# Layer 2 attention: the transposed sums go ahead of the weighted sums in the first step of a query block

## The chip, the cores and the metric

The kernel runs on one core of a Trainium2 chip. The metric is the device time of one execution in microseconds; the time of a kernel is the median over several executions. A core has five engines with instruction queues of their own: TensorE (PE in the profile, with its weight loads listed apart as PEld), VectorE (DVE), ScalarE (ACT), GpSimdE (POOL) and SyncE (SP, which here only issues DMAs). Each engine runs its queue in order; semaphores make one engine wait for another.

## The reference, cut to what matters

The program is a stack of four layers over x of 8 images of 56 x 56 positions with 128 channels. The change lies in the attention of layer 2, where each image is 3136 tokens. Keys, queries and values are the same projection, so that the matrix of scores is symmetric.

```
kqv = x @ W_k.T
h = kqv.reshape(B, S, HEADS, D_K).transpose(0, 2, 1, 3)      # 8 heads of 16
scores = jnp.einsum('bhqd,bhkd->bhqk', h, h) / jnp.sqrt(jnp.float32(D_K))
attn = jax.nn.softmax(scores, axis=-1)
ctx = jnp.einsum('bhqk,bhkd->bhqd', attn, h)
ctx = ctx.transpose(0, 2, 1, 3).reshape(B, S, D)
t = t + ctx @ W_o.T
```

After it come a normalization, the gate and the choice of tokens for the experts, which the kernel does in the same stage.

## The kernel before, in words

The function `attend` holds the stage. Its order is written out by hand (a manual schedule): each engine gets its instructions in the order in which the code below issues them.

The work is cut into 16 parts `u`: 8 images times 2 groups of four heads. Within a part there are 8 query blocks `b`, taken from 7 down to 0; each is 384 queries wide (`QB`), and block 7 is 448. The keys are cut into tiles of 128; three tiles (`KB`) make a key block `a`. A step is one query block against one key tile, and there are 1856 steps: in each part 25 for block 7 and 13 for each of the blocks 6 to 0.

Because the scores are symmetric, a square of exponentials that was computed for queries `b` and keys `a` serves the pair the other way round too, once it is transposed. So each square is computed once and used twice:

- `scores` (line L1252 of the profile) makes the scores of a step: four matmuls, one for each head, into two of three PSUM buffers `p_s`; ScalarE takes the exponential of each half into `e` (L1260).
- `weigh` (L1305) multiplies the exponentials with the values: four matmuls into the PSUM tile `av`, summed over all the steps of the block. These are the weighted sums. The pool of `av` has one buffer.
- `transpose_squares` (L1271) has VectorE transpose the 32 x 32 squares of `e` into `sq`; `move_squares` (L1287) then issues twelve DMAs on SyncE that move them to other partitions in `x`, and `keep_squares` (L1298) has GpSimdE copy the four that stay on theirs. Each key block so moved is a job.
- `from_squares` multiplies one third of a job with the values: four matmuls, again by `weigh` and so again on L1305, into the PSUM tile `avx`. These are the transposed sums. A job is begun `AGE` = 6 steps after it was made and takes three steps. The tile `avx` shares its one PSUM buffer with the small products of the finishing work (`p_o`, `p_tr`, `p_g`, `p_pool`).
- `take` has VectorE add `av` or `avx` to the block's accumulator (L1324; L1326 and L1328 where it is the first).
- `finish` is the work on a finished block: normalization, the product with W_o (`p_o`, L1366), the transposes (`p_tr`, L1404, evicted on L1405), the gate (`p_g`, L1408, evicted on L1409). It is a generator, advanced one piece in a step by `go_on`.

One matmul of float32 is two instructions in the profile, so that each group of four shows as x8 there.

Within a step `i` the code issues, in this order: the scores of step `i + 1`; the transposes of step `i`; two copies on GpSimdE; perhaps one piece of finishing work; perhaps the next block's queries; the weighted sums of step `i`; if the block ends here, the take of `av`; one third of a job, if one is due; and the DMAs of a job that is complete. So on TensorE a step is: scores, perhaps a small product, weighted sums, transposed sums.

A block's first step (`opens`) begins a new sum in `av`. There the weighted sums must wait until VectorE has taken the last block's sum out of the same PSUM buffer. There are 128 such steps. In 127 of them a job's third is due, by the order of the code: in 111 the first third of a job (the one that waits for the job's DMAs, for GpSimdE's copies and for the buffer of `avx`), in 16 the second third (all in the first step of block 6).

Of the kernel before, what the change touches and what calls it, by code (L numbers as in the profile page):

```python
# [53 lines left out]
AGE = 6  # L54
# [1100 lines left out]
def attend(tc, k, w, low, tok, kT_in, va_in, t_out, gate_w, gate_b, taken, pooled):  # L1155
# [11 lines left out]
    with ExitStack() as ctx:  # L1167
# [23 lines left out]
        def stage(b):  # L1191
            own = [(b, i, m) for i, (_, m) in enumerate(blocks[b][2])]
            if b == last:
                others = [3, 2, 1, 6, 5, 4, 0]
            else:
                others = [(b - r) % last for r in (3, 2, 1)]
                own.append((NQ, 0, S - 128 * (KT - 1)))
            for r, a in enumerate(others):
                yield from [(a, i, 128) for i in range(KB)]
                n_own = -(-len(own) // (len(others) - r))  # L1200
                yield from own[:n_own]
                del own[:n_own]

        steps = [
            (u, b, *step)
            for u in range(len(parts))
            for b in reversed(range(NQ))
            for step in stage(b)
        ]
        keys, queries, exps, squares, sums = {}, {}, {}, {}, {}  # L1210
        jobs, moves, urgent, later = [], [], [], []
# [25 lines left out]
        def make_queries(u, b):  # L1237
            kT, width = keys[u, b][0], blocks[b][1]
            q = wp.tile([128, QB + 64], F32, name="q", bufs=2)
            nc.vector.tensor_scalar(in_order(q), by_square(kT), low, None, ALU.add)  # L1240
            if width > QB:
                nc.vector.tensor_scalar(q[:, QB:width], kT[:, QB:], low, None, ALU.add)
            queries[u, b] = q

        def scores(u, b, a, i, m):

            kT, q, width = keys[u, a][0], queries[u, b], blocks[b][1]
            e = ep.tile([128, 4, QB + 64], F32, name="e")
            ss = [pss.tile([128, 2, 512], F32, name="p_s") for _ in range(2)]
            for j in range(4):  # L1250
                rows = slice(32 * j, 32 * j + 32)
                nc.tensor.matmul(  # L1252
                    ss[j // 2][:m, j % 2, :width],
                    kT[rows, 128 * i : 128 * i + m],
                    q[rows, :width],
                    start=True,
                    stop=True,
                )
            for j in range(2):
                nc.scalar.activation(  # L1260
                    e[:m, 2 * j : 2 * j + 2, :width], ss[j][:m, :, :width], AF.Exp
                )
            exps[u, b, a, i] = e

        def transpose_squares(u, b, a, i):

            if i == 0:
                squares[u, b, a] = tp.tile([128, 4, KB, 4, KB * 32], F32, name="sq")
            sq = squares[u, b, a]
            for j in (0, 2):  # L1270
                nc.vector.transpose(  # L1271
                    sq[:, :, i, j : j + 2].rearrange("p s j c -> p j s c"),
                    exps[u, b, a, i][:, j : j + 2, :QB].rearrange(
                        "p j (s c) -> p j s c", s=4
                    ),
                )

        def move_squares(u, b, a, now):

            sq = squares.pop((u, b, a)).rearrange("p s a j c -> p s (a j c)")  # L1280
            x = xp.tile([128, 4, KB * 4 * KB * 32], F32, name="x")

            for src, dst in (
                *((0, 1), (2, 3), (1, 0), (3, 2), (0, 2), (2, 0)),
                *((0, 3), (2, 1), (1, 2), (3, 0), (1, 3), (3, 1)),
            ):
                nc.sync.dma_start(  # L1287
                    x[32 * dst : 32 * dst + 32, src], sq[32 * src : 32 * src + 32, dst]
                )
            for at in range(4):  # L1290
                rows = slice(32 * at, 32 * at + 32)
                moves.append((x[rows, at], sq[rows, at]))
            jobs.append([u, b, a, x.rearrange("p s (a f) -> p (s a) f", a=KB), 0, now])

        def keep_squares():

            for _ in range(min(2, len(moves))):
                nc.gpsimd.tensor_copy(*moves.pop(0))  # L1298

        def weigh(av, u, b, i, m, e, start, stop):  # L1300
            for j in range(4):
                out = av[32 * j : 32 * j + 32]
                if len(e[j].shape) == 3:
                    out = out.rearrange("p (a i) -> p a i", i=32)
                nc.tensor.matmul(out, keys[u, b][1][:m, i, j, :], e[j], start=start, stop=stop)  # L1305

        def from_squares():
            u, b, a, x, i, _ = jobs[0]
            assert not (i == 0 and len(jobs) == 1 and moves)
            if i == 0:  # L1310
                sums[0] = psm.tile([128, QB], F32, tag="m", name="avx")
            e = [x[:, :, (KB * j + i) * 32 : (KB * j + i) * 32 + 32] for j in range(4)]
            weigh(sums[0], u, b, i, 128, e, i == 0, i == KB - 1)
            jobs[0][4] += 1
            if i == KB - 1:
                jobs.pop(0)
                take(u, a, sums[0])

        def take(u, b, av):

            width = blocks[b][1]
            to = by_square(acc[b])
            if done[b]:
                nc.vector.tensor_tensor(to, to, in_order(av), ALU.add)  # L1324
            else:
                nc.vector.tensor_copy(to, in_order(av))  # L1326
                if width > QB:
                    nc.vector.tensor_copy(acc[b][:, QB:], av[:, QB:width])  # L1328
            done[b] += 1
            if done[b] == (1 if b == last else 5):  # L1330
                work = [finish(*parts[u], b), False]
                urgent.append(work)
                later.append(work)
# [83 lines left out]
        def go_on(work):  # L1417
            try:
                work[1] = next(work[0])
            except StopIteration:  # L1420
                later.remove(work)
# [4 lines left out]
        def reload():  # L1426

            while loads:
                u, b = loads[0]
                n = u - 1  # L1430
                if b < NQ and (
                    not {(n, b), *((n, (b + r) % last) for r in (1, 2, 3) if b < last)} <= used
                    or any(j[:2] == [n, b] for j in jobs)
                ):
                    return
                load_keys(*loads.pop(0))
# [7 lines left out]
        for i, (u, b, a, c, m) in enumerate(steps):  # L1444
            if i + 1 < len(steps):
                scores(*steps[i + 1])
            if a < NQ and a != b:
                transpose_squares(u, b, a, c)
            keep_squares()
            free = not jobs or jobs[0][4] == 0  # L1450
            if urgent:
                go_on(urgent.pop(0))
            elif later and i > turn + 1 and (free or not later[0][1]):
                go_on(later[0])
                turn = i
            if i + 3 < len(steps) and steps[i + 3][:2] != steps[i + 2][:2]:
                make_queries(*steps[i + 3][:2])
            opens = i == 0 or steps[i - 1][:2] != (u, b)
            closes = i + 1 == len(steps) or steps[i + 1][:2] != (u, b)
            if opens:  # L1460
                av = psa.tile([128, 512], F32, tag="av", name="av")
            e = exps.pop((u, b, a, c))
            width = blocks[b][1]
            weigh(
                av[:, :width],
                u,
                a,
                c,
                m,
                [e[:m, j, :width] for j in range(4)],  # L1470
                opens,
                closes,
            )
            if closes:
                take(u, b, av)
                used.add((u, b))
            if jobs and (i - jobs[0][5] >= AGE or i + 1 == len(steps)):
                from_squares()
            if a < NQ and a != b and c == KB - 1:
                move_squares(u, b, a, i)  # L1480
            reload()
# [698 lines left out]
def token_layers(tc, k, a, y, out):  # L2180
# [3 lines left out]
    with ExitStack() as ctx:  # L2184
# [57 lines left out]
        with tc.If(taken > 0) as both:  # L2242
            attend(tc, k, w, low, tok, kT_d, va_d, *dest)
# [100 lines left out]
```

## Time and profile before

| what | value |
|---|---|
| time, median of 3 runs | 7714.85 us (7708.21 to 7727.53) |
| the profiled execution's own time | 7718.14 us |
| its span, first to last instruction | 7716.3 us |
| busy share of the span: PE, DVE, ACT, POOL | 84%, 68%, 54%, 38% |
| the stage of `attend` | from about 1965 us to about 6500 us |
| L1252 scores, PE | 14848 instructions, 548 ns mean |
| L1305 weighted sums into `av`, PE | 14848 instructions, 515 ns mean |
| L1305 transposed sums into `avx`, PE | 10752 instructions, 496 ns mean |
| L1260 exponentials, ACT | 3712 instructions, 830 ns mean |
| L1271 transposes, DVE | 2688 instructions, 950 ns mean |

How to read it: the four matmuls of a group run side by side in the array, and the next group starts before the last has drained, so that the sum of the instructions' times says little; what counts on TensorE is the distance from the start of one group to the start of the next. "Idle" of PE is time in which no matmul was in flight; "idle" of PEld is time between two weight loads, in which matmuls may well be running. PEclk is the share of its clock that TensorE was granted, 1.00 or 0.50 in this stage.

### The profile page before, as it was taken

The page shows a single profiled execution, that of the slowest core. Times are in us where ns is not written, and L with a number is a line of the kernel's source. Part 1 is how long each engine was busy: PE and PEld are TensorE (multiplying, and loading weights), DVE is VectorE, ACT ScalarE, POOL GpSimd, SP SyncE. Part 2 cuts the span into 40 slices and gives each one's busy share as a digit, 9 for nine tenths or more (in the row PEclk, how much of TensorE's full clock was granted, in tenths as well). Part 3 has the DMA queues.
Part 4 walks back from the last instruction along what each step waited for, and adds up shares of the span by engine and source line. Part 5 has one row for each costly group of instructions (what it writes and reads, how often), then busy time and mean ns, then how long its engine had stood idle before and what let it go on. Part 6 is the DMA issues. An engine that isn't in the chain of part 4 may idle for free. (4 is left out here: it accounts for less than half of the span.)

```text
span 7716.3 us, 157926 instructions
## 1 busy us (share of the span) xinstructions
PE 6482.3 (84%) x59883; PEld 2880.7 (37%) x59883; DVE 5284.8 (68%) x9856; ACT 4142.6 (54%) x6467; POOL 2935.1 (38%) x2555
## 2 busy tenths in 40 slices
PE   6659999556899999999999999999999997556654
PEld 4446666334233323323323323333333333245532
DVE  7975564366677777777777777777777776366752
ACT  4424444122666666666666666666666664056740
POOL 0011111022444444444444444444444443434653
PEclk8768898777999999999999999999999998788766
DMA  5453443376788778778778778778778775543543
GB/s 155 137 119 76 86 95 65 82 240 207 199 203 197 193 192 199 189 192 201 191 184 204 188 183 207 183 191 205 185 190 206 182 190 137 196 117 107 134 135 130
DMA packets 736303, 1287.38 MB, mean 167 GB/s; under 512 B 117698, under 2 KB 503108, under 8 KB 728516
## 3 DMA queue, kind: packets, MB, share of 16 engines
q1 hardware_dynamic: 725556, 1260.76, 65.1%
q0 software_dynamic: 6144, 12.60, 0.6%
q8 instruction: 484, 7.93, 0.5%
q10 hardware_dynamic: 3824, 3.68, 0.2%
q14 instruction: 295, 2.42, 0.1%
HBM read 286.04 MB, written 197.81 MB: 63 GB/s over the span
## 5 line engine op out<-in xcount | busy, mean ns | idle before, releaser
L1260 ACT ACTIVATE e<-p_s 128x768 f32<-128x768 f32 (+2 forms) x3712 | 2887.8, 830 | 1584.9 <-PE p_s L1252 1329.8
L1298 POOL COPY x<-sq 32x1152 f32<-32x1152 f32 x1792 | 2059.2, 1149 | 2067.6 <-PE p_s L1252 1330.0
L1271 DVE STREAM_TRANSPOSE sq<-e 128x768 f32<-128x768 f32 x2688 | 2434.5, 950 | 567.3 <-ACT e L1260 312.9
L1252 PE MATMUL p_s<-q,kT 32*128 32x384 f32 (+2 forms) x14848 | 1888.6, 548 | 33.6 <-ACT e L1260 18.6
L1305 PE MATMUL av<-e,va 128*32 128x384 f32 (+2 forms) x14848 | 1645.3, 515 | 30.4 <-DVE acc L1324 20.7
L1305 PE MATMUL avx<-x,va 128*32 128x384 f32 x10752 | 1138.3, 496 | 69.5 <-issue 40.2
L1252 PEld LDWEIGHTS p_s<-q,kT 32*128 32x128 f32 (+1 forms) x14848 | 654.8, 181 | 1252.6 <-issue 825.4
L1305 PEld LDWEIGHTS av<-e,va 128*32 128x32 f32 (+1 forms) x14848 | 294.5, 108 | 1049.4 <-issue 941.7
L1305 PEld LDWEIGHTS avx<-x,va 128*32 128x32 f32 x10752 | 353.2, 111 | 650.9 <-issue 595.2
L609 POOL TENSOR_TENSOR rs<-rs,mhalf 112x4 f32<-112x4 f32 x112 | 116.1, 1036 | 788.3 <-DVE rs L608 788.3
L1324 DVE TENSOR_TENSOR acc<-acc,avx 128x384 f32<-128x384 f32 x336 | 183.9, 547 | 229.9 <-PE avx L1305 228.6
L121 PE MATMUL p_tr<-ident,xn 112*128 112x112 f32 x672 | 134.6, 341 | 187.4 <-DVE xn L112 141.8
L1141 POOL TENSOR_TENSOR rs<-rs,mhalf 112x4 f32<-112x4 f32 (+2 forms) x136 | 168.1, 1236 | 269.3 <-DVE ntop L1942 123.8
L525 ACT COPY wT<-p_w 88x448 f32<-88x448 f32 x152 | 138.0, 922 | 194.1 <-PE p_w L523 161.4
L1990 ACT ACTIVATE xn<-t,ms,rs 112x128 f32<-112x128 f32 x448 | 185.3, 488 | 76.4 <-DVE ms L1983 76.4
L327 DVE SCALAR_TENSOR_TENSOR acc<-xp,dw,acc 128x3136 f32<-128x3136 f32 x56 | 194.3, 3478 | 31.3 <-ACT acc L322 31.2
L637 PE MATMUL p_f<-x1T,w 128*128 128x448 f32 x448 | 205.6, 583 | 4.4 <-DVE x1T L632 2.7
L121 PEld LDWEIGHTS p_tr<-ident,xn 112*128 112x128 f32 x672 | 98.7, 169 | 285.0 <-issue 185.1
L1385 POOL TENSOR_TENSOR rs<-rs,mhalf 128x3 f32<-128x3 f32 (+1 forms) x72 | 58.5, 815 | 365.0 <-DVE rs L1384 343.0
L523 PE MATMUL p_w<-ident,wide 112*88 112x112 f32 x896 | 146.5, 303 | 58.6 <-DMA px<-strips 34.1
L621 DVE TENSOR_TENSOR y<-y,p_rs 128x448 f32<-128x448 f32 x112 | 69.3, 619 | 176.6 <-PE p_rs L614 176.6
L122 ACT COPY xT<-p_tr 128x448 f32<-128x448 f32 x112 | 59.6, 532 | 229.8 <-PE p_tr L121 203.7
(354 smaller groups left out, 7830.9 us busy)
## 6 DMA issues: line engine op xcount, KB each, us to landing
x<-sq SPq DMA_DIRECT2D x5376, 144.0 KB
w<-in_L_ffn_weight_dram SPq DMA_DIRECT2D x64, 1024.0 KB
px<-strips SPq DMA_DIRECT2D x64, 616.0 KB
va_d<-va SPq DMA_DIRECT2D x16, 1600.0 KB
xT_d<-xT SPq DMA_DIRECT2D x112, 224.0 KB
xT<-xT_d SPq DMA_DIRECT2D x112, 224.0 KB
kT_d<-kT SPq DMA_DIRECT2D x16, 1568.0 KB
t<-t_a SPq DMA_DIRECT2D x16, 1568.0 KB
```

Of the source, the lines that this page charges most:

```text
L121: nc.tensor.transpose(p[:, i, :], src[:, i, :], k.ident[:T, :T])
L327: nc.vector.scalar_tensor_tensor(acc, xp[:, j // 3 : j // 3 + IH, j % 3 : j % 3 + IW], dw[:, j : j + 1], acc, ALU.mult, ALU.add,)
L523: nc.tensor.transpose(p[:, g], around[:, :, g], k.ident[:T, :T])
L637: nc.tensor.matmul(p, q.w1[:, f * 128 : (f + 1) * 128], x1T, start=True, stop=True)
L1141: nc.gpsimd.tensor_tensor(rs, rs, k.mhalf[:m, :n], ALU.pow)
L1252: nc.tensor.matmul(ss[j // 2][:m, j % 2, :width], kT[rows, 128 * i : 128 * i + m], q[rows, :width], start=True, stop=True,)
L1260: nc.scalar.activation(e[:m, 2 * j : 2 * j + 2, :width], ss[j][:m, :, :width], AF.Exp)
L1271: nc.vector.transpose(sq[:, :, i, j : j + 2].rearrange("p s j c -> p j s c"), exps[u, b, a, i][:, j : j + 2, :QB].rearrange("p j (s c) -> ...
L1298: nc.gpsimd.tensor_copy(*moves.pop(0))
L1305: nc.tensor.matmul(out, keys[u, b][1][:m, i, j, :], e[j], start=start, stop=stop)
L1324: nc.vector.tensor_tensor(to, to, in_order(av), ALU.add)
L1990: nc.scalar.activation(out[:, i], x[:, i], AF.Identity, bias=ms[:, i : i + 1], scale=rs[:, i : i + 1])
```

## The change

In the first step of a block (but the very first of all), if a job's third is due, `from_squares` is called before the weighted sums and no longer after them. In all other steps nothing is changed. On TensorE the four transposed matmuls and the four weighted ones change places in 127 steps; on the other engines the order of the instructions stays as it was. The number of instructions of computation stays the same.

```diff
             if opens:
+
+                if i and jobs and i - jobs[0][5] >= AGE:
+                    from_squares()
                 av = psa.tile([128, 512], F32, tag="av", name="av")
...
-            if jobs and (i - jobs[0][5] >= AGE or i + 1 == len(steps)):
+            if jobs and not opens and (i - jobs[0][5] >= AGE or i + 1 == len(steps)):
                 from_squares()
```

## The prediction

> **What bounds the kernel now.** The change touches only the stage of `attend`, so I read the table of busy time for that stretch first, then the waits of TensorE, then its timeline around the first steps of blocks.
>
> ```profile
> 1965.00:6500.00 4535.00, 4370.16 (x41569) 1436.31 (x41568) 3411.62 (x4905) 2918.07 (x3814) 2146.77 (x1894) 0.98 0.80 193
> ```
>
> The columns are the stretch, its length, the busy time of PE, PEld, DVE, ACT and POOL, the granted clock, the DMA share and GB/s. TensorE is busy for 4370 of 4535 us and sets the pace: all its idle time is 165 us, and what the change can win is a part of that.
>
> Which part, the waits of that stretch tell (engine, line, releaser: us in total, times, longest). First those of PE, then the one row of PEld that names the same releaser.
>
> ```profile
> PE avx L1305 <- issue: 40.2, 38, 2.2
> PE av L1305 <- DVE acc L1324: 20.7, 15, 2.4
> PE av L1305 <- DVE acc L1328: 8.8, 16, 0.6
> ```
>
> ```profile
> PEld av L1305 <- DVE acc L1324: 74.1, 96, 3.1
> ```
>
> The row of 74.1 us looks like the larger prize and is none: weight loads sit idle while the matmuls before them run. In matmuls the weighted sums lose 20.7 + 8.8, about 30 us in 31 openings. What the other 96 openings look like, a plain one shows (timeline of PE: start, length, line, names, count, idle before and its releaser):
>
> ```profile
> 2947.24 0.94 PE L1252 MATMUL p_s<-q,kT 32*128 32x384 f32 x8
> 2948.11 0.85 PE L1305 MATMUL av<-e,va 128*32 128x384 f32 x8
> 2948.78 0.85 PE L1305 MATMUL avx<-x,va 128*32 128x384 f32 x8
> 2949.57 0.91 PE L1252 MATMUL p_s<-q,kT 32*128 32x384 f32 x6
> ```
>
> From group to group: scores to weighted 0.87 us, weighted to transposed 0.67 us, transposed to scores 0.79 us, with no wait. VectorE has freed `av` before the scores are through. These starts are the prices of the groups: a moved group fills at most some 0.7 us (0.78 in block 7, whose rows are wider).
>
> **The change, part by part.** Only TensorE's order differs, in 127 openings; no DMA is moved, and the queues of SP, POOL, ACT and DVE keep theirs. I went through all 127 in the timeline and sorted them.
>
> *Block 6, 16 openings.* The weighted sums wait for the second copy of block 7's take, L1328:
>
> ```profile
> 2559.69 1.13 PE L1252 MATMUL p_s<-q,kT 32*128 32x384 f32 x8
> 2561.39 0.85 PE L1305 MATMUL av<-e,va 128*32 128x384 f32 x8 [0.57 <-DVE acc L1328]
> 2562.03 0.85 PE L1305 MATMUL avx<-x,va 128*32 128x384 f32 x8
> ```
>
> The moved group is here a job's second third, which waits for nothing. It takes the 0.57 us and the weighted group follows when the buffer is free. Gain 16 x 0.55 = 8.8 us.
>
> *Block 7, 8 openings with a short wait.* Seven wait 0.50 us for L1324, one 0.66: gain 4.2 us.
>
> *Block 7, 7 openings with a long wait.* In them VectorE works on the choice of tokens:
>
> ```profile
> 2783.94 1.15 PE L1252 MATMUL p_s<-q,kT 32*128 32x448 f32 x8
> 2787.46 1.72 PE L1305 MATMUL av<-e,va 128*32 128x448 f32 x8 [2.37 <-DVE acc L1324]
> ...
> 2800.67 0.64 PE L1706 MATMUL p_pool<-expert,chosen 128*128 128x64 f32 x2 [2.19 <-DVE chosen L112]
> ```
>
> The moved group fills 0.78 of the 2.37 us, 5.5 us in all, if TensorE kept it. But 13 us on it waits another 2.2 us for VectorE, and VectorE is idle for only 0.56 us in between. What is won first is mostly waited for later. Between 0 and 5.5 us I take 3 us, near the 7 x 0.56 that VectorE can pass on.
>
> *The plain 74 openings.* Here nothing is hidden that was not hidden before, but the transposed sums now need their input 0.67 us earlier. GpSimdE's copies are done 5.5 us or more ahead in all of them. The DMAs are not: the records of TensorE's semaphore instructions and the ends of the packets put the last piece of a job within some 0.7 us of the weighted group's start in 13 openings. There the transposed group would start 0.1 to 0.95 us late, and the weighted one behind it. Summed one by one: 6 us lost. The bounds are 0, if these pieces come just in time, and 74 x 0.67 = 50 us, if the DMAs keep the pace at every opening; I stay with the sum, because it is read from these very openings. The change of neighbours costs little: weighted to scores takes 0.78 us in steps without transposed sums, against 0.76 for transposed to scores, so 127 x 0.02 = 2.5 us.
>
> *Openings with a gate product, 15, in blocks 5 and 4.* Here the change does harm:
>
> ```profile
> 2625.94 1.10 PE L1252 MATMUL p_s<-q,kT 32*128 32x384 f32 x8
> 2626.97 0.86 PE L1408 MATMUL p_g<-xT,gate 128*64 128x384 f32 x2
> 2627.76 0.85 PE L1305 MATMUL av<-e,va 128*32 128x384 f32 x8
> 2629.26 0.85 PE L1305 MATMUL avx<-x,va 128*32 128x384 f32 x8 [0.64 <-issue]
> 2630.04 0.93 PE L1252 MATMUL p_s<-q,kT 32*128 32x384 f32 x8
> ```
>
> `p_g` and `avx` share one PSUM buffer. `avx` starts 0.10 us after VectorE's eviction on L1409 ends at 2629.16, and that eviction stands behind two transposes (L1271) in VectorE's queue. Today the weighted sums run inside that wait. After the change they are queued behind it on TensorE, with the next scores behind them, and ScalarE's next exponentials wait for those. The transposed group cannot start earlier; the weighted one comes after it: 15 x 0.67 = 10.1 us lost.
>
> *Openings with a transpose, 7, in block 3.* The same with `p_tr` and its eviction on L1405: the transposed group already waits 1.38 us behind the weighted one. The loss is 0.67 less the 0.13 us that the weighted group waits today: 3.8 us.
>
> *The clock.* Idle time has a second price. The long wait above lies in the first of these two stretches (columns as in the table above):
>
> ```profile
> 2783.69:2787.10 3.41, 1.40 (x12) 0.43 (x8) 3.20 (x12) 2.86 (x4) 1.83 (x2) 1.00 0.90 210
> 2787.10:2790.51 3.41, 3.05 (x20) 0.71 (x20) 3.34 (x6) 0.00 (x0) 3.30 (x3) 0.50 0.95 224
> ```
>
> After a stretch in which TensorE was idle for 2.0 of 3.41 us the clock is 0.50 for the next 3.41 us. The stage has 39 such dips, and their starts lie on one grid of 3.41 us. Laying that grid over the stage: all 28 stretches with 1.9 us idle or more are followed by a dip, of those between 1.45 and 1.9 about half, below 1.45 none. A dip takes half of 3.41 us, 1.7 us. In the gate openings the idle stretch grows from about 0.4 to 1.1 us, harmless, but in three it comes to about 1.4 and in one to 2.3: two new dips, to be generous. In block 3 five of seven dip already; with 0.67 us more, all do: two more. Four dips are 6.8 us. That block 7's long waits fall from 2.37 to about 1.6 us may save dips, but what they save is waited for at `p_pool`; I count nothing (the far end is 7 x 1.7 = 12 us gained).
>
> The Trainium skill has a rule on this ("TensorE: Matmul & The Clock Gate", section "Why this matters for your kernels"): no idle gaps over about 3 us between bursts of matmuls. By it no opening here could dip, before or after, and the sum would be 6.8 us smaller. The row above speaks against that threshold: the gap of 2.37 us was enough.
>
> **The sum.** Gains 8.8 + 4.2 + 3 = 16.0. Losses 10.1 + 3.8 + 6 + 2.5 + 6.8 = 29.2. Net 13 us slower: 7718.1 of the profiled execution becomes 7731, and on the median of the runs, 3.3 us lower, 7714.9 + 13 = 7728. A difference of 0.3%, 23 us, is about what a measurement of this kernel can tell from no change; so my forecast is no change, with a lean to slower. With the unknowns at their near ends (no late pieces, no new dips: 0; twice of both: +26) its own range is 7706 to 7738.
>
> **The rivals.**
>
> *The new wait is dearer* (slower, over 0.3%). One mechanism: the wait for the shared PSUM buffer in the 22 openings with a gate product or a transpose, now with nothing in front of it, lengthens TensorE's idle past the point where the clock halves. It decides from 1.9 us idle in one stretch of the grid. If all 15 gate openings dip, not two, that is 13 x 1.7 = 22 us more: 7750. For it: five of seven transposes dip today, at 1.5 to 1.9 us. Against it: 1.1 us in eleven of the fifteen. Chance 0.30.
>
> *The DMAs keep the pace.* All 74 plain openings wait out the 0.67 us: 50 in place of 6, 7772. For it: the DMA share of 0.80 and the 13 late openings. Against it: half of the pieces have landed 1.8 us before. Chance 0.06.
>
> *The gains stand alone* (faster). If evictions came earlier, and block 7 kept its fill and its dips: 8.8 + 4.2 + 5.5 + 12 = 30 us, 7685. Against it: the order on VectorE doesn't change, so the eviction can't come earlier. Chance 0.07.
>
> *The waits row is right.* Whoever adds PEld's 74.1 to the 30 expects 104 us: 7611. The plain opening speaks against it. Chance 0.01.
>
> **How the numbers follow.** No change within 0.3% (7692 to 7738) 0.56; slower 0.30 + 0.06 = 0.36; faster 0.07 + 0.01 = 0.08. The range of 7700 to 7760 takes in the forecast and the dearer wait and leaves out most of the DMA case and of the faster ones.
>
> **What would show it.** Right: the waits of `av` on L1328 and the short ones on L1324 are gone from PE's list; the wait of `avx` in the gate openings is about 0.7 us longer, for the same eviction; block 7's long waits are split, and `p_pool` waits longer; `avx` waits for `x<-sq` in about a dozen plain openings; some 40 dips in the stage. Wrong: a PE idle sum in the stage that moves by more than 25 us, dips that change by more than ten, or waits in steps that are not openings.

## The result, and the profile after

Measured side by side, 14 runs of each, the changed kernel takes 7741.2 us (7727.4 to 7768.6) and the kernel before 7707.6 us: ratio 1.0041, 95% interval 1.0032 to 1.0051, so about 32 us slower (33.6 us by the medians). The time lies in the stated range (7700 to 7760). It lies outside the forecast's own range (7706 to 7738) and beyond the 0.3%: the class that came true is "slower", to which the prediction gave 0.36.

The profiled execution of after took 7744.67 us, its span is 7742.8. Reckoned from the first scores to the last weighted group, the stage of `attend` takes 4555.8 us; before it took 4525.7. So the stage that the change touches is 30.1 us longer, and the two profiled executions differ by 26.5: all of the difference lies in that stage. The stretch in which the prediction read TensorE's busy time, here 20 us longer so that it ends about where the stage does (columns as there):

```profile
1965.00:6520.00 4555.00, 4373.69 (x41537) 1438.85 (x41535) 3412.80 (x4901) 2918.78 (x3815) 2147.41 (x1894) 0.98 0.79 192
```

TensorE is busy for 4374 us, as it was for 4370; the other engines' sums stay within 2.5 us. The new time is idle time of TensorE: 181 us against 165. Which, its waits tell (engine, line, releaser: us in total, times, longest):

```profile
PE avx L1305 <- issue: 50.3, 43, 2.3
PE p_pool L1709 <- DVE chosen L112: 24.2, 7, 3.5
PE p_s L1252 <- ACT e L1260: 22.2, 15, 2.5
PE avx L1305 <- DVE xT L1405: 16.6, 7, 2.4
PE av L1305 <- DVE acc L1324: 11.1, 7, 1.6
```

What the change aimed at has happened: the wait of `av` for L1328 (8.8 us) is off the list, and that for L1324 went from 20.7 us in 15 to 11.1 us in 7. But the other rows grew: `avx` for issue from 40.2, `p_pool` from 14.6, `p_s` for the exponentials from 18.6 in 9, `avx` for L1405 from 9.7. `avx` waits 9.5 us for the DMAs, from 6.4.

**Block 6.** The opening that the prediction showed, in the timeline of TensorE after:

```profile
2562.27 1.14 PE L1252 MATMUL p_s<-q,kT 32*128 32x384 f32 x8
2563.34 0.85 PE L1305 MATMUL avx<-x,va 128*32 128x384 f32 x8
2564.01 0.83 PE L1305 MATMUL av<-e,va 128*32 128x384 f32 x8
```

The gap of 0.57 us is gone, and from these scores to the next it is 2.49 us instead of 3.13.

**A gate opening**, the same as in the prediction:

```profile
2630.95 0.85 PE L1305 MATMUL avx<-x,va 128*32 128x384 f32 x8 [1.40 <-issue]
2631.59 0.85 PE L1305 MATMUL av<-e,va 128*32 128x384 f32 x8
```

The transposed group waits 1.40 us in place of 0.64, for the same eviction (it starts 0.10 us after the end of L1409, as before), and the weighted group, which used to run inside that wait, stands behind it.

**A transpose opening**, in the timeline, and the two stretches of the clock's grid around it:

```profile
4960.45 1.51 PE L1305 MATMUL avx<-x,va 128*32 128x384 f32 x8 [2.37 <-DVE xT L1405]
4961.70 1.53 PE L1305 MATMUL av<-e,va 128*32 128x384 f32 x8
```

```profile
4956.48:4959.89 3.41, 1.26 (x11) 0.34 (x3) 3.41 (x6) 1.81 (x3) 3.33 (x3) 1.00 1.01 237
4959.89:4963.30 3.41, 2.85 (x20) 0.81 (x20) 2.19 (x4) 0.00 (x0) 0.09 (x1) 0.50 0.99 235
```

The wait was 1.38 us before. TensorE is now idle for 2.15 of the first 3.41 us and has a clock of 0.50 in the next, so that both groups take 1.5 us instead of 0.85. All seven openings of this kind are followed by such a dip; before, five were.

**Block 7, a long wait**, the same opening as in the prediction: the weighted group and, later, `p_pool`; then the stretch from the opening's scores to `p_pool`, first of before, then of after (columns as in the stretches above):

```profile
2792.32 0.96 PE L1305 MATMUL av<-e,va 128*32 128x448 f32 x8 [1.58 <-DVE acc L1324]
...
2805.52 1.63 PE L1709 MATMUL p_pool<-expert,chosen 128*128 128x64 f32 x8 [3.45 <-DVE chosen L112]
```

```profile
2783.94:2800.67 16.73, 12.18 (x101) 3.47 (x97) 15.68 (x32) 9.52 (x12) 9.71 (x9) 0.90 0.90 236
```

```profile
2788.80:2805.52 16.72, 11.69 (x100) 3.27 (x96) 16.23 (x32) 9.51 (x12) 9.70 (x9) 1.00 0.89 232
```

The wait at the opening fell from 2.37 to 1.58 us and the dip after it is gone (clock 1.00 instead of 0.90). Yet the stretch has the same length to 0.01 us: `p_pool` waits for the same chain of VectorE, 3.45 us instead of 2.19. VectorE is busy for 16.23 of the 16.72 us, where it was busy for 15.68 of 16.73: it has lost its idle time and finishes no sooner. The reason stands in one product of the normalization, L1350, and in the copy that GpSimdE makes at the same moment. First before, then after:

```profile
2797.03 0.82 DVE L1350 TENSOR_TENSOR by_q<-by_q,r 128x384 f32<-128x384 f32 x1
```

```profile
2796.29 1.14 POOL L1298 COPY x<-sq 32x1152 f32<-32x1152 f32 x1
```

```profile
2801.20 1.50 DVE L1350 TENSOR_TENSOR by_q<-by_q,r 128x384 f32<-128x384 f32 x1
```

```profile
2801.15 1.14 POOL L1298 COPY x<-sq 32x1152 f32<-32x1152 f32 x1
```

The product starts 12.40 us after the opening's scores instead of 13.09, and ends 13.90 us after them both times, 0.41 us behind the end of the copy, which stands at the same place in both. So it is in all seven of these stretches: the product starts 0.65 to 0.88 us earlier and ends at the same place to 0.01 us.

By kind of step, from the start of a step's scores to the next step's, after less before (parts are counted from 0 to 15, here and below):

| steps | us |
|---|---|
| openings of block 6 (16) | -10.3 |
| openings of block 7, even parts (7) / odd parts (8) | -2.9 / -12.0 |
| openings with a gate product (15) | +9.5 |
| openings with a transpose (7) | +8.2 |
| plain openings (74) | +6.5 |
| all other steps of block 6 / block 7 | +16.6 / +11.2 |
| all other steps of the other blocks, closing steps | +2.9, +0.4 |

All openings together come to about zero (-1.0). The loss stands in steps that the change does not touch, of the very blocks in which it wins: block 6 as a whole is 6.3 us longer, block 7 only 3.2 us shorter.

### The profile page after: what moved, and what is told of

Same layout as the page of the kernel before. It is cut to its first block, busy times and chain, and to the rows that moved or that the text cites. A ratio compares the mean times of both kernels' runs of the same rounds, so it can differ in the third digit from the quotient of the medians.

```text
span 7742.8 us, 158015 instructions
## 1 busy us (share of the span) xinstructions
PE 6477.2 (84%) x59883; PEld 2884.0 (37%) x59883; DVE 5286.1 (68%) x9856; ACT 4143.5 (54%) x6467; POOL 2936.6 (38%) x2555
## 5 line engine op out<-in xcount | busy, mean ns | idle before, releaser
L1298 POOL COPY x<-sq 32x1152 f32<-32x1152 f32 x1792 | 2060.2, 1150 | 2092.0 <-PE p_s L1252 1365.6
L1305 PE MATMUL av<-e,va 128*32 128x384 f32 (+2 forms) x14848 | 1647.4, 515 | 11.1 <-DVE acc L1324 11.1
L1324 DVE TENSOR_TENSOR acc<-acc,avx 128x384 f32<-128x384 f32 x336 | 183.7, 547 | 230.2 <-PE avx L1305 229.1
```

## The experiments

My theory after the result had two parts. The shared PSUM buffer costs some 20 us in the 22 openings with a small product. And what blocks 6 and 7 win is given back a few steps later. The rivals: the new order is bad as such, wherever it stands; or the clock's dips cost the time; or the gain in blocks 6 and 7 is real and other openings lose more than they seem to. All ratios are to the kernel before, run on the same chip.

### The change in three parts

**Blocks 6 and 7 alone** (31 openings).

```diff
+            first = opens and i > 0 and (b >= 6)
...
+                if first and jobs and i - jobs[0][5] >= AGE:
+                    from_squares()
...
-            if jobs and (i - jobs[0][5] >= AGE or i + 1 == len(steps)):
+            if jobs and not first and (i - jobs[0][5] >= AGE or i + 1 == len(steps)):
```

> The transposed sums go first in 31 openings alone, those of blocks 6 and 7, where the weighted sums waited for VectorE before. Theory (VectorE sets the pace there, so that what TensorE wins in the opening it waits for two or three steps later): between 3 us faster and 6 us slower than the kernel before, with the waits of av gone and those of p_o, p_pool or avx in the next steps longer. Rival (the gain is kept): 13 to 16 us faster.

Measured: 7725.8 us against 7718.3, ratio 1.0010 (1.0001 to 1.0019). The stage takes 4525.8 us in its trace, as before the change. The openings win 24.4 us (9.6 and 14.9), the steps between openings and ends lose 25.7; `p_pool` waits 24.2 us as in after. So the gain is real at the openings and not kept; by the medians the kernel is 7.5 us slower, a little more than the 6 that I allowed. The rival by which this part would be faster falls.

**The openings with a small product alone** (22). `psm.n` counts the tiles that the finishing work has taken from the pool of the shared buffer, `small` is its value at the start of the step; the rest of the edit is as above.

```diff
+            first = opens and i > 0 and (psm.n > small)
```

> The transposed sums go first in 22 openings alone, those in which a gate product or a transpose was put into the shared PSUM buffer in the same step. Theory (the weighted sums now stand behind the wait for its eviction): 14 to 20 us slower, all of it in these 22 steps. Rival (each of these waits also halves the clock): 35 us slower or more, with some 15 more dips. Rival (later waits shrink in return): within 5 us.

Measured: 7746.8 us, ratio 1.0041 (1.0028 to 1.0054). In the trace the stage is 18.7 us longer: gate openings +10.2, transpose openings +10.2, all other steps between openings and ends together -0.7. The time says 32 us (22 to 42), more than the stage shows; this profiled execution was 22.9 us longer than that of before, and what lies between is not explained. There are 35 dips in the stage against 37, so the rival in which every gate opening dips falls. Openings that the edit does not touch repeat within 1.3 us here and within 2.2 us in the next run; sums over the other steps of a block or of a group of blocks differ by up to 6.4 us where nothing was changed, which tells how far such sums can be trusted.

**The plain openings alone** (74).

```diff
+            first = opens and i > 0 and (b < 6 and psm.n == small)
```

> The transposed sums go first in the 74 plain openings alone, where nothing waited before. Theory (a dozen of them now wait for the last DMA of their job): 6 to 10 us slower. Rival (the DMAs keep the pace): 50 us. Rival (nothing happens here): within 3 us.

Measured: 7724.7 us, ratio 1.0009 (1.0000 to 1.0017); the stage takes 4525.6 us. The plain openings lose 8.1 us, all of it in 16 of the 74 (57 are as long as before to 0.05 us); other steps win 9.6. So these openings cost a few us at most, and the DMAs do not keep the pace at every one of them.

The parts come to 0.1 + 18.7 + 0.0 = 18.8 us in the stage, the whole to 30.1. The missing 11 us lie in steps that no edit touches, where such sums scatter. By the medians of the runs it is the other way round: the parts cost 7.5 + 28.5 + 6.4 = 42.4 us, the whole 33.6.

### Is it the shared buffer, or the order as such?

**The kernel before, with small products only while no third is due.** A step's small product, and the transposed sums that need its buffer, then no longer meet.

```diff
-            free = not jobs or jobs[0][4] == 0
+            free = not jobs or (jobs[0][4] == 0 and i - jobs[0][5] < AGE)
```

> The kernel before, but a piece of finishing work that needs the shared PSUM buffer is issued only in steps in which no third of a job is due. If the waits of avx for that buffer are on the path that sets the end, the rows of before (avx by issue 40 us, by xT 10 us) put it at 20 to 50 us faster. Rival (the finishing work slips and is done at the end with nothing beside it, or VectorE is the pace there): the same, or slower.

Measured: 7707.9 us against 7718.3, ratio 0.9991 (0.9982 to 1.0000). I had expected more. No gate or transpose opening is left, but the finishing work is late, and the choice of tokens makes TensorE wait in 28 places instead of 7 (27.1 us at `p_pool`).

**After, with small products kept out of an opening alone.**

```diff
+            due = bool(jobs) and i - jobs[0][5] >= AGE
+            first = i > 0 and steps[i - 1][:2] != (u, b)
-            free = not jobs or jobs[0][4] == 0
+            free = not jobs or (jobs[0][4] == 0 and not (first and due))
```

> The changed kernel, but in a first step in which a third of a job is due no finishing work that needs the shared PSUM buffer is issued; the 22 small products slip to a later step. Theory (the loss is the weighted sums behind the eviction of that buffer): about 20 us faster than the changed kernel, so within 10 us of the kernel before. Rival (the loss comes from the moved order as such): it stays 30 us slower than the kernel before.

Measured: 7681.7 us against 7710.0, ratio 0.9968 (0.9956 to 0.9979). Against the trace of after the stage is 57.3 us shorter, and the openings that had held a gate product or a transpose account for it: -32.0 and -30.8 us, plain openings +5.8, other steps -1.9. With the same order of weighted and transposed sums the kernel is now 28 us faster than the one before, so the order is no harm in itself. Part of that comes from moving the products, whatever the order; the next run holds that part fixed.

**After, with the rule of the kernel before the last.**

```diff
-            free = not jobs or jobs[0][4] == 0
+            free = not jobs or (jobs[0][4] == 0 and i - jobs[0][5] < AGE)
```

> The changed kernel with the small products only in steps in which no third of a job is due at all. Theory: as the kernel before with the same rule (7 us faster than the kernel before) plus what the blocks 6 and 7 and the plain openings cost alone, 0 to 15 us: within 10 us of the kernel before. Rival (the change costs 30 us in itself): 20 us slower or more.

Measured: 7665.9 us against 7710.0, ratio 0.9947 (0.9934 to 0.9959). Its stage is 30.2 us shorter than with the same rule and the order of before: plain openings -11.4, block 6's -8.2, block 7's -6.5, closing steps -5.2. Under this rule, the same on both sides, the change that cost 30 us of stage wins 30: the harm in the small openings is the buffer that a product shares with `avx`, not the order. The size of this gain is not that of the order alone: 18.9 of the 30 us lie in block 3, where the rule had cost the old order 12.6 us, so that the new one also fills waits that the rule brought in. Neither my expectation (within 10 us of the kernel before) nor the rival saw a gain of 44 us coming. (The two kernels ran on different chips, each beside the kernel before; the ratios differ by 0.44%.)

### Who takes the gain of block 6 back?

In part 3 the whole chain can be read. The opening's scores start at 2853.87 us before and at 2857.36 after. The transposes of the opening step's squares, which VectorE makes while TensorE is in the second step, first before, then after:

```profile
2857.16 1.84 DVE L1271 STREAM_TRANSPOSE sq<-e 128x768 f32<-128x768 f32 x2 [1.74 <-DMA x<-sq]
```

```profile
2860.94 1.84 DVE L1271 STREAM_TRANSPOSE sq<-e 128x768 f32<-128x768 f32 x2 [2.17 <-DMA x<-sq]
```

The exponentials of ScalarE that need the buffer `e` which those transposes empty, and the second half of the scores of TensorE's third step, both of after:

```profile
2862.87 1.51 ACT L1260 ACTIVATE e<-p_s 128x768 f32<-128x768 f32 x2 [3.04 <-DVE sq L1271]
```

```profile
2863.73 0.91 PE L1252 MATMUL p_s<-q,kT 32*128 32x384 f32 x4 [0.82 <-ACT e L1260]
```

TensorE begins the third step 0.77 us earlier after its opening's scores than before (4.63 instead of 5.40 us). But VectorE cannot begin the transposes earlier: their buffer `sq` is still being read by the DMAs. They start 3.58 us after the opening's scores, not 3.29; ScalarE's exponential follows, then TensorE's second half of the scores, and the weighted group of the third step comes 7.22 us after the opening's scores, where it came 6.93 us after them. The DMAs are issued by SyncE, here in part 2 of after:

```profile
2528.43 33.89 SPq L1287 DMA_DIRECT2D x<-sq  x48
...
2563.39 7.48 SPq L1287 DMA_DIRECT2D x<-sq  x12
```

A job's twelve take 7.48 us here, and from there to 9.2 us over all jobs of after; the three steps of block 7 in which the next job is made take 7.5 us on average. The row of 48 is four jobs. SyncE paused in it for 0.5 and 1.6 us before the second and the third, whose transposes were not done, but not before the fourth, whose last DMA it issued as the opening of block 6 began. It is this fourth job that the transposes of the opening step wait for, since they write into its buffer. In all 16 parts of before and of after SyncE goes over to this job within 0.5 us, and the transposes start 1.9 to 3.7 us after its last DMA was issued, 0.3 us or more after the exponentials that they read were done. So SyncE works at its limit just before the opening of block 6, and nothing that TensorE does in the opening can make it earlier. The weighted group of the third step then follows 3.64 to 3.70 us after the start of the transposes in seven of the eight odd parts, before as after. The other candidate was the finishing work on VectorE, which in the even parts makes TensorE wait at `p_o` in this same step.

**The kernel before, with no finishing work in the first four steps of block 6.**

```diff
+            if i and steps[i - 1][:2] != (u, b):
+                begun = i
+            hold = b == last - 1 and i - begun < 4
-            if urgent:
+            if urgent and not hold:
...
-            elif later and i > turn + 1 and (free or not later[0][1]):
+            elif later and not urgent and i > turn + 1 and (free or not later[0][1]):
```

> The kernel before, but in the first four steps of block 6 the normalization of block 7 on VectorE, and all other finishing work with it, is held back. Theory (VectorE sets the pace there): the waits of p_o and of avx for VectorE in the third step of block 6 shrink, and the time is 10 to 30 us less. Rival (the work only slips to where VectorE is as full): the same.

Measured: 7671.5 us against 7710.0, ratio 0.9951 (0.9938 to 0.9963). This is more than I expected. Block 6 is 66.5 us shorter (the stage as a whole 46.2, as other blocks lose by it), the wait of `p_o` for L1326 (18.2 us) is gone.

**The same with the new order in blocks 6 and 7** (the edit of the first experiment).

> The same with the transposed sums first in the 31 openings of blocks 6 and 7. Theory: with VectorE relieved, block 6 keeps its gain, some 9 us less in block 6 than the kernel that only holds the work back; without the relief block 6 kept nothing. Rival (something else than VectorE gives it back): block 6 is no faster than there.

Measured: 7677.3 us, ratio 0.9962 (0.9949 to 0.9974). The openings of block 6 win 9.9 us, and the block is still 2.9 us longer. No finishing work stands there any more, so the theory that VectorE's finishing work takes the gain back fell. What is left is the wait for the DMAs: VectorE's waits for `x<-sq` in these steps grow from 7.9 to 13.0 us. In the three parts where they grow most (by 2.3, 3.1 and 1.2 us) the block is 1.2, 1.8 and 1.4 us longer by its fourth step; in the part where one of 2.1 us vanishes, 1.1 us shorter. The name hides some of it. The transposes wait for up to eight DMA semaphores and two others, and the profile puts the wait down to one of them, in some parts to `t<-tok` or to exponentials that had ended 0.6 us or more before. Part 6, 1.0 us longer, has no wait named `x<-sq`, but one named `t<-tok` before the same transposes, 0.67 us without the new order and 2.23 with it. Under any name VectorE stands idle before these transposes in 15 of the 16 parts, 17.9 us in sum without the new order and 22.6 with it; and with it the third step's weighted group comes 3.64 us after their start in the same 15 parts, however early the opening was done.

**That kernel's base with the jobs of block 7 further apart.** The tiles of block 7's own keys, which make no job, are put behind the last four of the other key blocks and no longer behind the first four, so that its last jobs lie four steps apart instead of three.

```diff
+                if b == last and r < len(others) - len(blocks[b][2]):
+                    continue
```

> The kernel that holds the finishing work back in block 6, with block 7's own four key tiles moved to the end of its steps, so that its last jobs lie four steps apart and not three. It is the partner of the next run. Theory (the transposes of block 6 wait for the DMAs that empty their buffer): VectorE's waits for x<-sq at the start of block 6 are gone; the time is 5 us less to 5 us more than without the move.

Measured: 7783.9 us against 7713.3, ratio 1.0090 (1.0075 to 1.0104). I had taken this for neutral and it is not: block 7 is 123 us longer than in its base, and `p_pool` alone makes TensorE wait 46.4 us. As a base for the next run it serves: of VectorE's waits for `x<-sq` in the first steps of block 6 not one is left in 16 parts, and the transposes start 4.1 us or more after the last DMA out of their buffer was issued.

**The same with the new order in blocks 6 and 7.**

> The same with the transposed sums first in the 31 openings of blocks 6 and 7. Theory (what block 6 wins in its opening is waited for two steps later because the transposes wait for the DMAs out of their buffer, and the exponentials for the transposes): with the DMAs done earlier block 6 keeps the gain, some 8 us less in block 6 than its partner. Rival (the give-back has another source): block 6 is no shorter than in its partner, as it was without the move of the key tiles.

Measured: 7777.8 us, ratio 1.0084 (1.0069 to 1.0099). Only seven of the even parts test it (2 to 14), as in the others the weighted group has no wait to fill. There the opening is 0.65 us shorter and the block stays so to 0.01 us: 5.0 us in all, where I had expected 8.

The five pairs side by side: how much later (+) or earlier (-) some points of block 6 come after its opening's scores with the new order, in us, summed over the 16 parts, and how much the time at half clock in its first four steps changes.

| pair | third step's scores | its weighted group | fourth step's scores | fifth's | at half clock |
|---|---|---|---|---|---|
| before, after | -10.3 | +0.9 | +4.3 | +8.2 | +24.3 |
| blocks 6 and 7 alone | -9.6 | +1.2 | +1.9 | +6.6 | +13.8 |
| no finishing work there | -9.9 | +1.3 | +2.2 | +2.9 | +2.8 |
| jobs further apart | -5.0 | -5.0 | -5.0 | -5.0 | 0.0 |
| both rules (below) | -15.3 | -13.8 | -13.8 | -13.8 | -13.4 |

In the first three the whole gain is gone within one step, at the weighted group that waits for the exponentials. With the finishing work there, dips of the clock add to it. With no DMA to wait for, all of it stays. That the DMAs out of the transposes' buffer take the gain is read from the traces in nearly all parts; by an experiment that removes the wait it is shown for these seven parts alone, in a base that differs in block 7; a third buffer of `sq`, the direct test, has no room in SBUF and wasn't tried.

### Both remedies together

**The kernel before with both rules** (small products only while no third is due; no finishing work in the first four steps of block 6), **and the changed kernel with both.** The edits are those above.

> The kernel before with both rules for the finishing work: small products only in steps in which no third of a job is due, and none of it in the first four steps of block 6. Each alone measured 7 and 38 us faster than the kernel before; if they add, 45 us faster, if the slipped work meets VectorE elsewhere, 30 us.

> The changed kernel with both rules. Theory (the change hurts only through the shared PSUM buffer, and with that out of the way it wins, as it did with the first rule alone, 44 against 7 us): 20 to 40 us faster than its partner, 60 to 85 us faster than the kernel before. Rival (the change is no gain, and the 37 us between the two with the first rule came from where the slipped work fell): within 10 us of its partner.

Measured: 7683.3 us, ratio 0.9961 (0.9947 to 0.9975), and 7655.3 us, ratio 0.9926 (0.9912 to 0.9940), both against 7713.3. The two rules do not add: with the old order they win 30 us together, no more than the second alone. The last kernel is the best of all: 28 us faster than its partner, as expected, 58 us faster than the kernel before (a little less than the 60 to 85 expected), some 1.1% faster than the changed kernel. In it the change is worth 25.3 us of stage.

In the opening of block 6 in part 9, for one, VectorE is behind with the choice of tokens, and `av` waits 2.36 us for L1328; with the new order it waits 1.58 us, the moved group takes the other 0.78, and the time at half clock in these steps falls by 13.4 us in the 16 parts. The gain of block 6 lies in the odd parts, in which VectorE's wait for `x<-sq` in these steps is 0.5 us in one and nothing in the others, and all but 1.5 of its 15.3 us stay. In part 1, where VectorE does stand idle before those transposes (1.4 and 1.6 us, named after the exponentials), the 0.64 us won are lost by the third step's weighted group.

## Why the prediction was right and wrong

**Right: what bounds the stage, and that the openings would lose about what they win.** The rows that the prediction named moved as it said, the PEld row of 74.1 us was no prize, and the sum over all openings is -1.0 us.

**Right: the shared buffer.** Gate openings 10.1 us forecast, 9.5 measured (10.2 alone). Transpose openings 3.8 us and two dips of 1.7, together 7.2; measured 8.2 (10.2 alone), with seven dips instead of five as said. The two dips allowed for the gate openings came to one. Terms of 20.7 us together, measured 17.7 in after and 20.4 alone.

**Right: the late DMAs.** 6 us in 13 plain openings by the records of before; in after 14 of the 74 are longer by 0.15 us or more, by 6.3 us in sum, and alone 16, by 8.1. The further 2.5 us for the change of neighbours are not there: 57 of the 74 are as long as before to 0.05 us, in after as well as in the run with these openings alone.

**Wrong: the gains of 16 us.** Here is the step that failed: "It takes the 0.57 us and the weighted group follows when the buffer is free. Gain 16 x 0.55 = 8.8 us." The opening did win that, 10.3 us. But I booked it as kept, and asked only for block 7's long waits what is late next. The answer for block 6 lay in VectorE's rows of before: its transposes in the block's second step wait for the DMAs out of `sq`. Block 6 came to +6.3 us where -8.8 stood. For block 7 the sum had -7.2 and the stage shows -3.2; in its odd parts the openings won 12.0 us, dips included, and all but 1.8 went to later waits, as the stretch of 16.7 us shows. I took 3 us there, near the 0.56 us of idle time that VectorE was to pass on in each, and it was nearer to the lower end, 0: that idle time went into the product on L1350, which ended with GpSimdE's copy and no sooner, an engine that the prediction had not asked about here. The three terms together are off by 16.0 + 3.1 = 19.1 us; the other terms came out some 5 us cheaper than forecast and untouched steps 3 dearer, which gives the 17 us between 13 and 30. One of the prediction's own signs of being wrong came true: waits in steps that are not openings.

**Wrong: the own range.** It varied the dips and the late pieces only, from 0 to +26 us. On 7714.9 this is 7715 to 7741; the 7706 to 7738 that stands there does not follow from it. The measured difference, some 32 us, lies above. Had the gains been given a bound at nothing kept, it would have reached 7744.

**The rivals.** The dearer wait with many more dips is not what happened, although the time is close to its 7750, and it is by luck that the time fell into the range that was stretched for this rival. The stage has 37 dips before and after. But eight of them and no longer five last for two stretches of the grid, so that the time at half clock grows from 150.8 to 162.4 us; half of the difference, about 6 us, is near the 6.8 that the prediction had put down to new dips. And they moved: time at half clock fell from 31.4 to 8.8 us in the first four steps of block 7 and rose from 33.8 to 58.0 us in those of block 6 and from 17.1 to 27.3 us in those of block 3. The Trainium skill ("TensorE: Matmul & The Clock Gate", section "Why this matters for your kernels") asks for idle gaps of no more than about 3 us; the transpose opening above, with no single gap over 2.37 us, halved the clock, so here the measurement decides against it again. The rival in which the gains stand alone fell with the first experiment, the one in which the DMAs keep the pace with the third.

**Open.** Whether the 11 us between the three parts and the whole are more than the scatter of single traces; why untouched steps win 9.6 us when only the plain openings change; why the openings with small products alone cost 32 us of time and 18.7 of stage.

## What to carry to other kernels

A wait that is filled on the pacing engine is worth only what the next wait behind it does not take: before booking it, follow the engines that feed the next two or three steps, down to the queue that issues their DMAs and to the copies of GpSimdE, and put the lower bound of every gain at nothing. Before an operation is moved forward, look at what else uses its buffer at that point; if a product of other work does, move that first. The same edit cost 30 us in one schedule and won 25 to 30 us in two others whose collisions had been taken out.

## What the runs showed of the hardware

The number of dips can stay the same (37) while they wander and grow longer: a gap filled in block 7 took 22.6 us at half clock from its first four steps, and those of block 6, which follows it, got 24.2 us more. A DMA of `x<-sq` costs SyncE some 0.62 us of issue (7.48 us for twelve), so that a queue that looks like a mere helper can be the bound of three steps of 2.5 us. One and the same instruction of VectorE, the product on L1350 of 128x384 float32, takes 0.56 us where no copy of GpSimdE (L1298) runs beside it and up to 1.53 us where one does: in the traces of before and after, all 163 that started 0.16 us or more before the end of such a copy ended 0.405 to 0.414 us after it, whenever they had started.
